# The third block's shared up products by seven products of eight, in a decoder layer kernel

## The chip, the cores and the metric

The kernel runs on one core of one Trainium2 chip, in fp32 throughout. The metric is the device time of one execution in microseconds (us), as a median of several runs. The engines are TensorE (PE, products; PEld is its loading of weights), VectorE (DVE), ScalarE (ACT), GpSimd (POOL) and SyncE (SP, which issues most transfers). Products land in PSUM, which PE writes and DVE and ACT read.

## The reference, cut to what matters

The program is one decoder layer on x of 8 sequences of 256 rows and 256 features, 2048 rows in all: causal self attention with 16 heads; three rounds of a GRU whose input is an attention over a context of 120 rows; and a feed-forward part with one shared expert and eight routed ones, of which each row uses two. A layer norm follows each. The change is in the shared expert:

```
def _mlp(x, w1, b1, w2, b2):
    h = gelu(einsum('bsd,di->bsi', x, w1) + b1)
    return einsum('bsi,id->bsd', h, w2) + b2
...
return x + _mlp(x, sh_w1, sh_b1, sh_w2, sh_b2) + moe_out
```

w1 is 256 x 1024 and w2 is 1024 x 256. The gelu is the tanh form.

## The kernel before, in words

Rows are worked on in 4 blocks of 512 (`X[i]`), with their transposed copies `XT[i]`: 128 partitions, 2 chunks of features (`dc`), 512 rows. In the shared expert a unit u is half a block, 256 rows, so units 4 and 5 are the third block, i = 2.

`up` (L1223) makes the hidden values of one unit: for each of 8 slices c of the hidden dimension, two products of 128x128 weights by 128x256 rows add into PSUM, and ACT takes the sum out with gelu and bias into `hT` (L1241). Two slices share one PSUM tile of the pool "big", which has two buffers of two banks each. `down_group` (L1244) adds 8 products over the slices for 128 rows into a tile of the pool "bk" (four buffers). `shared_up`, `shared_down` and `parts` call these for the shared expert. The pool of `hT` has two buffers.

Around it stand these parts, in order of time. `place` (L1047) computes for each row the slots of its two experts, and POOL scatters the rows into a table `xd` with indirect transfers, 8 per block (L1070). `tables` works out which expert each tile of gathered rows has. The shared units 0 to 3 follow. Then comes the loop over 21 tiles of routed rows (`tile_fetch`, `tile_weights`, `tile_turn`, `tile_up`, `tile_down`, `tile_store`), whose results go to a table `yd`, and a branch for two rare tiles that is skipped when they are empty. The tail does the shared units 4 to 7. In it `fetch_back(i)` has POOL gather the two expert rows of each row of block i (8 indirect transfers, L1365, into 16 buffers `y`), `take_back(i)` has DVE add them with their weights to `Z[i]` (8 operations, L1379), and `finish` does the last layer norm and the store:

```
shared_up(4)
fetch_back(0)
shared_up(5)
fetch_back(1)
take_back(0)
parts(4)
take_back(1)
shared_up(6)
```

The order of PE and ACT is as written throughout (`manual_schedule`). In the tail DVE and POOL are as written too. Between the first stage and the tail, DVE and POOL are ordered by a scheduler, which can move an instruction ahead of earlier ones that are not ready: the additions of the shared bias for units 4 to 7 (L1268), written just ahead of the expert loop, run at 677 to 682 us, before the routing of the last two blocks.

`wih_sb` and `whh_sb` (128 partitions, 2 x 768 values each) hold the GRU's weights. Before these are loaded they hold sums for the query and key projections of the attention, which are already done by seven products of eight (`project_part`), as are the value projections (`product`); the additions of products there are on DVE (L392, L466), the sums of operands on POOL (L307). PE last reads `wih_sb` at about 395 us and `whh_sb` at 661 us.

Of the kernel before, what the change touches and what calls it, by code (L numbers as in the profile page):

```python
# [10 lines left out]
F32 = mybir.dt.float32  # L11
I32 = mybir.dt.int32
U16 = mybir.dt.uint16
AF = mybir.ActivationFunctionType
ALU = mybir.AluOpType
# [6 lines left out]
NE, FF = 8, 1024  # L22
P = 128
DC = D // P
# [5 lines left out]
FC = FF // P  # L30
# [7 lines left out]
RT = 256  # L38
# [27 lines left out]
def decoder_kernel(  # L66
# [23 lines left out]
    nc = tc.nc  # L90
# [6 lines left out]
    def big(name):  # L97
        return pools["big"].tile([P, 2, 512], F32, tag="big", name=name)

    def bank(name):  # L100
        return pools["bk"].tile([P, 512], F32, tag="bk", name=name)
# [13 lines left out]
    XT = [act.tile([P, DC, BLK], F32, tag=f"XT{i}", name=f"XT{i}") for i in range(NBLK)]  # L115
# [52 lines left out]
    b1c = vec_sb[:, 0 : (NE + 1) * FC].rearrange("p (e c) -> p e c", c=FC)  # L168
# [10 lines left out]
    wih_sb = const.tile([P, DC, 3 * D], F32, name="wih_sb")  # L179
    whh_sb = const.tile([P, DC, 3 * D], F32, name="whh_sb")  # L180
# [28 lines left out]
    def load_shared():  # L209
        w1_sb = sh.tile([P, DC, FF], F32, name="sh1")  # L210
        w2_sb = sh.tile([P, FC, D], F32, name="sh2")
        nc.sync.dma_start(w1_sb, sh_w1.rearrange("(c p) f -> p c f", p=P))
        nc.sync.dma_start(w2_sb, sh_w2.rearrange("(c p) d -> p c d", p=P))
        return w1_sb, w2_sb
# [56 lines left out]
    with (  # L271
# [34 lines left out]
        def minus(o, a, b, op=ALU.subtract):  # L306
            nc.gpsimd.tensor_tensor(o, a, b, op)  # L307
# [335 lines left out]
        for k in range(last + 1):  # L643
            i, j = divmod(k, 2 * NPAIR)
# [46 lines left out]
    shared = load_shared()  # L691
# [8 lines left out]
    fh = ctx.enter_context(tc.tile_pool(name="fh", bufs=2, side="right"))  # L700
# [51 lines left out]
    for h in range(2):  # L752
        n = (NSINGLE + 1 - h) // 2
# [12 lines left out]
    def tt(o, a, b, op):  # L766
        nc.vector.tensor_tensor(o, a, b, op)  # L767
# [452 lines left out]
    f1 = ctx.enter_context(tc.tile_pool(name="f1", bufs=1))  # L1220
    wff = ctx.enter_context(tc.tile_pool(name="wff", bufs=2))

    def up(w1_sb, bias, rhs, name, width=RT, between={}):  # L1223

        hT = fh.tile([P, FC, RT], F32, tag="hT", name=f"hT_{name}")
        for c2 in range(FC // 2):
            between.get(c2, nothing)()
            ph = big(f"ph_{name}_{c2}")
            for a in range(2):
                c = 2 * c2 + a  # L1230
                for dc in range(DC):
                    nc.tensor.matmul(  # L1232
                        ph[:, a, 0:width],
                        w1_sb[:, dc, ts(c, P)],
                        rhs(dc),
                        start=dc == 0,
                        stop=dc == DC - 1,
                    )
            for a in range(2):
                c = 2 * c2 + a  # L1240
                nc.scalar.activation(hT[:, c, 0:width], ph[:, a, 0:width], AF.Gelu_apprx_tanh, bias=bias[:, c : c + 1])  # L1241
        return hT

    def down_group(po, w2_sb, hT, a):  # L1244
        for c in range(FC):
            nc.tensor.matmul(po, hT[:, c, ts(a, P)], w2_sb[:, c, :], start=c == 0, stop=c == FC - 1)  # L1246

    def down(w2_sb, hT, name, between=nothing, groups=RT // P):
        po = bank(f"pf_{name}").rearrange("p (a b) -> p a b", b=D)
        for a in range(groups):  # L1250
            if a:
                between()
            down_group(po[:, a, :], w2_sb, hT, a)
        return po
# [3 lines left out]
    HT = {}  # L1258

    def shared_up(u, between={}):  # L1260
        i, h = divmod(u, BLK // RT)
        rhs = lambda dc: XT[i][:, dc, ts(h, RT)]
        HT["s", u] = up(shared[0], b1c[:, NE, :], rhs, f"s{u}", between=between)

    def shared_bias(u):

        i, h = divmod(u, BLK // RT)
        nc.vector.scalar_tensor_tensor(  # L1268
            Z[i][:, ts(h, RT // P), :],
            X[i][:, ts(h, RT // P), :],  # L1270
            2.0,
            shared_b.unsqueeze(1).to_broadcast([P, RT // P, D]),
            ALU.mult,
            ALU.add,
        )

    def shared_down(u):

        i, h = divmod(u, BLK // RT)
        if u < SHARED_FIRST:  # L1280
            shared_bias(u)
        hT = HT.pop(("s", u))
        po = bank(f"pf_s{u}").rearrange("p (a b) -> p a b", b=D)
        down_group(po[:, 0, :], shared[1], hT, 0)
        yield
        down_group(po[:, 1, :], shared[1], hT, 1)
        z = Z[i][:, ts(h, RT // P), :]
        tt(z, z, po, ALU.add)
        yield
# [55 lines left out]
    def tile_down(t):  # L1345
        row = TI.pop(t)[0]
        w1_sb, w2_sb, bt, b2t, e = TW.pop(t)
        n = groups(t)
        po = down(w2_sb, HT.pop(("t", t)), f"t{t}", groups=n)
        yo = f2.tile([P, 2, D], F32, tag="yo", name=f"yo_{t}")[:, 0:n, :]  # L1350
        tt(yo, po[:, 0:n, :], b2t.unsqueeze(1).to_broadcast([P, n, D]), ALU.add)
        return row, yo
# [6 lines left out]
    def fetch_back(i):  # L1359

        for n in range(NSUB):
            for j, slot in enumerate(slots):
                g = i * NSUB + n
                y = f2.tile([P, D], F32, tag="y", name=f"y_{g}_{j}", bufs=NY)
                nc.gpsimd.indirect_dma_start(  # L1365
                    out=y,
                    out_offset=None,
                    in_=yd[:, :],
                    in_offset=bass.IndirectOffsetOnAxis(ap=slot[:, g : g + 1], axis=0),
                )  # L1370
                Y[g, j] = y
# [12 lines left out]

    nunit = NT // RT
    shared_up(0)
    place(1)
    residual(3)
    nc.scalar.preload_act_table_set(LNEXP)
    norm(2)  # L1390
    norm(3)
    part = [shared_down(u) for u in range(nunit)]

    def parts(u):
# [7 lines left out]

    route_logits(2, (0, 1))
    shared_up(
        1,
        {
# [14 lines left out]
    for u in range(2, SHARED_FIRST):  # L1421
        shared_up(u)
        if u == SHARED_FIRST - 1:
            tile_fetch(TILES[2])
            tile_weights(TILES[1])
            next(part[u])
            tile_turn(TILES[0])
            next(part[u])
        else:
            parts(u)  # L1430
    for u in range(SHARED_FIRST, nunit):
        shared_bias(u)


    with tc.manual_schedule(engines={mybir.EngineType.SP}):
        for k, t in enumerate(TILES):
# [5 lines left out]
            if k:  # L1442
                done = tile_down(TILES[k - 1])
# [19 lines left out]
    engines = {mybir.EngineType.PE, mybir.EngineType.Activation, mybir.EngineType.DVE, mybir.EngineType.Pool}  # L1463
    ctx.enter_context(tc.manual_schedule(engines=engines))
    half = NSUB // 2
    shared_up(4)
    fetch_back(0)
    shared_up(5)
    fetch_back(1)
    take_back(0)  # L1470
    parts(4)
# [16 lines left out]
    po = [bank(f"pf_s7_{a}")[:, 0:D] for a in range(half)]  # L1488
    hT = HT.pop(("s", 7))
    for a in range(half):  # L1490
        n = half + a
# [69 lines left out]
```

## Time and profile before

| | |
|---|---|
| median of 3 runs | 1056.69 us (1056.6 to 1056.99) |
| the profiled execution | 1092.43 us, its span 1090.4 us |
| PE busy | 1047.5 us, 96% of the span |
| DVE, ACT, POOL busy | 480.5, 422.9, 266.5 us |
| first product of unit 4's up | 1010.75 us |
| up of units 4 and 5 on PE | 14.05 us |
| POOL's gathers in the tail | 32, from 1014.28 us on |

All times of a view are us from the start of the span. A row of groups gives line, engine, operation, what it writes and reads with shapes, the count, then busy us and mean ns of one, and then how long the engine stood idle just before and what ended that. A row of the timeline gives start, length, engine, line, operation and count, and in brackets the idle time before it with its releaser. A row of the chain gives start, length and who worked. The trace records each fp32 product as two instructions, so a unit's 16 up products are x32. A product's record is longer than the step from one to the next, since they overlap in the pipeline: lengths of whole groups are used, not the mean of one.

### The profile page before, as it was taken

The page shows a single profiled execution, that of the slowest core. Times are in us where ns is not written, and L with a number is a line of the kernel's source. Part 1 is how long each engine was busy: PE and PEld are TensorE (multiplying, and loading weights), DVE is VectorE, ACT ScalarE, POOL GpSimd, SP SyncE. Part 2 cuts the span into 40 slices and gives each one's busy share as a digit, 9 for nine tenths or more (in the row PEclk, how much of TensorE's full clock was granted, in tenths as well). Part 3 has the DMA queues.
Part 4 walks back from the last instruction along what each step waited for, and adds up shares of the span by engine and source line. Part 5 has one row for each costly group of instructions (what it writes and reads, how often), then busy time and mean ns, then how long its engine had stood idle before and what let it go on. Part 6 is the DMA issues. An engine that isn't in the chain of part 4 may idle for free. (4 is left out here: it accounts for less than half of the span.)

```text
span 1090.4 us, 14560 instructions
## 1 busy us (share of the span) xinstructions
PE 1047.5 (96%) x5102; PEld 764.2 (70%) x5102; DVE 480.5 (44%) x1516; ACT 422.9 (39%) x1174; POOL 266.5 (24%) x314
## 2 busy tenths in 40 slices
PE   9999999999999999999999999959999999999877
PEld 5556766766676865555656667948888888888756
DVE  4567667766776362444434578510101010010137
ACT  2345555544467112555555444413223222221223
POOL 3734424444234032112121013330000000000650
PEclk9999999999999999999999999979999999999969
DMA  9000000000001089990000001153666766752231
GB/s 298 7 1 1 2 1 1 2 1 1 1 1 59 1 294 358 347 335 0 1 1 0 1 14 51 44 181 122 220 217 217 252 208 222 226 190 69 87 90 64
DMA packets 91368, 114.14 MB, mean 105 GB/s; under 512 B 6751, under 2 KB 82335, under 8 KB 91295
## 3 DMA queue, kind: packets, MB, share of 16 engines
q1 hardware_dynamic: 87135, 102.72, 28.8%
q0 software_dynamic: 3072, 8.39, 2.4%
q10 hardware_dynamic: 1088, 2.10, 0.5%
q8 instruction: 41, 0.67, 0.3%
q14 instruction: 32, 0.26, 0.1%
HBM read 67.97 MB, written 45.22 MB: 104 GB/s over the span
## 5 line engine op out<-in xcount | busy, mean ns | idle before, releaser
L503 ACT ACTIVATE sc<-sc,nmax 128x128 f32<-128x128 f32 (+1 forms) x256 | 113.3, 444 | 147.2 <-DVE nmax L490 147.2
L518 POOL TENSOR_TENSOR sc<-sc,sums 128x256 f32<-128x256 f32 (+1 forms) x128 | 103.2, 827 | 180.1 <-DVE sums L515 136.5
L1241 ACT ACTIVATE hT_t<-ph_t,bt 128x256 f32<-128x256 f32 (+1 forms) x168 | 66.3, 445 | 192.8 <-issue 138.3
L910 PE MATMUL gate<-XT,whh_sb 128*128 128x512 f32 x288 | 133.8, 593 | 0.0
L1232 PE MATMUL ph_t<-xgT,w 128*128 128x256 f32 (+1 forms) x672 | 132.5, 355 | 0.8 <-ACT hT_t L1241 0.8
L1246 PE MATMUL pf_t<-w,hT_t 128*128 128x256 f32 x592 | 131.1, 379 | 0.0
L1232 PEld LDWEIGHTS ph_t<-xgT,w 128*128 128x128 f32 x672 | 116.2, 190 | 14.8 <-ACT hT_t L1241 1.0
L1246 PEld LDWEIGHTS pf_t<-w,hT_t 128*128 128x128 f32 x592 | 111.0, 190 | 14.3
L1365 POOL DMA_INDIRECT y<-yd,slot x32 | 30.8, 961 | 308.8 <-ACT hT_s L1241 294.0
L910 PEld LDWEIGHTS gate<-XT,whh_sb 128*128 128x128 f32 x288 | 54.2, 189 | 48.5 <-issue 46.2
L392 DVE TENSOR_TENSOR qk<-pq,qk 128x256 f32<-128x256 f32 x168 | 64.7, 420 | 39.5 <-ACT qk L390 29.1
L490 DVE CUSTOM_DVE_ANT_0 sc<-pp,mask 128x128 f32<-128x128 f32 (+1 forms) x256 | 75.2, 349 | 8.6 <-PE pp L478 7.6
L1246 PE MATMUL pf_s<-sh,hT_s 128*128 128x256 f32 x256 | 61.3, 394 | 17.8 <-ACT hT_s L1241 11.6
L919 PEld LDWEIGHTS gate<-at,G 120*128 120x128 f32 x288 | 54.5, 189 | 29.9 <-issue 23.3
L919 PE MATMUL gate<-at,G 120*128 120x256 f32 x288 | 72.1, 379 | 0.4 <-DVE at L767 0.4
L1232 PE MATMUL ph_s<-XT,sh 128*128 128x256 f32 x256 | 62.1, 398 | 8.9 <-issue 6.8
L1337 DVE COPY xgT<-xg 128x512 f32<-128x512 f32 (+1 forms) x21 | 13.2, 628 | 128.5 <-PE xg L1336 128.5
L1246 PEld LDWEIGHTS pf_s<-sh,hT_s 128*128 128x128 f32 x256 | 50.0, 197 | 26.2 <-ACT hT_s L1241 12.0
L767 DVE TENSOR_TENSOR yo<-pf_t,b2t 128x512 f32<-128x512 f32 (+1 forms) x21 | 13.2, 628 | 121.5 <-PE pf_t L1246 121.5
L1241 ACT ACTIVATE hT_s<-ph_s,vec_sb 128x256 f32<-128x256 f32 x64 | 26.8, 471 | 96.3 <-PE ph_s L1232 54.0
L1232 PEld LDWEIGHTS ph_s<-XT,sh 128*128 128x128 f32 x256 | 50.2, 199 | 19.2 <-issue 9.8
L548 PE MATMUL po<-pT,v 128*64 128x256 f32 (+1 forms) x512 | 55.7, 339 | 2.6 <-ACT pT L537 2.6
(258 smaller groups left out, 1618.7 us busy)
## 6 DMA issues: line engine op xcount, KB each, us to landing
w<-in_ew_dram SPq DMA_DIRECT2D x42, 1024.0 KB, 5.6
xd<-zeros SPq DMA_DIRECT2D x1, 16640.0 KB, 54.8
yd<-zeros SPq DMA_DIRECT2D x1, 16640.0 KB, 103.2
xg<-xd SPq DMA_DIRECT2D x16, 256.0 KB, 5.1
yd<-yo SPq DMA_DIRECT2D x16, 256.0 KB, 5.8
b2t<-in_b_dram SPq DMA_DIRECT2D x21, 128.0 KB, 5.7
sh<-in_sh_w_dram SPq DMA_DIRECT2D x2, 1024.0 KB, 7.2
X<-in_x_dram SPq DMA_DIRECT2D x3, 512.0 KB, 11.6
```

Of the source, the lines that this page charges most:

```text
L392: nc.vector.tensor_tensor(o, pq[:, ts(n, S)], old, ALU.add)
L490: nc.vector.tensor_tensor_reduce(out=sc[:, h, seg[t]], in0=pp[h][:, seg[t]], in1=mask[:, seg[t]], scale=-(HD**-0.5), scalar=3.0e38, op0=AL ...
L503: nc.scalar.activation(sc[:, h, seg[t]], sc[:, h, seg[t]], AF.Exp, scale=-1.0, bias=nmax[:, t, h : h + 1], accum_out=sums[:, t, h : h + 1],)
L518: nc.gpsimd.tensor_tensor(sc[:, :, seg[t]], sc[:, :, seg[t]], sums[:, t, :].unsqueeze(2).to_broadcast([P, 2, w]), ALU.mult,)
L548: nc.tensor.matmul(po[ts(h, HD), q0:S], V[i][:, 2 * bi + c, ts(2 * pr + h, HD)], pT[:, h, 0:S] if c == 0 else pT[:, h, S:384], start=c == ...
L767: nc.vector.tensor_tensor(o, a, b, op)
L910: nc.tensor.matmul(pg[:, oc, :], whh_sb[:, dc, o], XT[i][:, dc, :], start=dc == 0, stop=not given and dc == DC - 1,)
L919: nc.tensor.matmul(pg[:, oc, ts(bi, S)], G[:, BPB * i + bi, o], AT_[p][:, bi, :], start=not hidden, stop=not hidden or bi == BPB - 1,)
L1232: nc.tensor.matmul(ph[:, a, 0:width], w1_sb[:, dc, ts(c, P)], rhs(dc), start=dc == 0, stop=dc == DC - 1,)
L1241: nc.scalar.activation(hT[:, c, 0:width], ph[:, a, 0:width], AF.Gelu_apprx_tanh, bias=bias[:, c : c + 1])
L1246: nc.tensor.matmul(po, hT[:, c, ts(a, P)], w2_sb[:, c, :], start=c == 0, stop=c == FC - 1)
L1365: nc.gpsimd.indirect_dma_start(out=y, out_offset=None, in_=yd[:, :], in_offset=bass.IndirectOffsetOnAxis(ap=slot[:, g : g + 1], axis=0),)
```

## The change

The two `shared_up` calls for block 2 are replaced by one `up_seven(2)`. The block's product is taken as 2 x 2 blocks: the weights by halves of the hidden dimension (512 wide) and the two chunks of features, the rows by the same two chunks and the two units. Seven products of sums of these blocks give the four results. `up_prepare(2)`, written after the shared biases and ahead of the expert loop, makes eight sums on POOL, s1 to s4 from the weights and t1 to t4 from the rows, in the space of `wih_sb` and `whh_sb`.

`up_seven` goes through four quarters q of 128 hidden values in each half. A quarter has two PSUM tiles of "big": x takes four products and y three. ACT copies the first product to SBUF (tile `c`, two buffers), DVE makes four additions of PSUM to `c`, and ACT takes the four results with gelu and bias into the `hT` of both units. `down_group` gets an order of slices, which for units 4 and 5 alternates between the halves. `fetch_back(0)` now stands after both units' up products, in the written order.

```
-    def down_group(po, w2_sb, hT, a):
-        for c in range(FC):
-            nc.tensor.matmul(po, hT[:, c, ts(a, P)], w2_sb[:, c, :], start=c == 0, stop=c == FC - 1)
+    def down_group(po, w2_sb, hT, a, order=range(FC)):
+        for n, c in enumerate(order):
+            nc.tensor.matmul(po, hT[:, c, ts(a, P)], w2_sb[:, c, :], start=n == 0, stop=n == FC - 1)
...
+    done = [w.rearrange("p k n -> p (k n)") for w in (wih_sb, whh_sb)]
+    up_sums = [done[0][:, ts(j, FF // 2)] for j in range(3)] + [done[1][:, 0 : FF // 2]]
+    half_sums = [done[1][:, FF // 2 + j * RT :][:, 0:RT] for j in range(4)]
+    up_blocks = [shared[0][:, k, ts(m, FF // 2)] for m in range(2) for k in range(DC)]
...
+    def up_prepare(i):
+        def minus(o, a, b, op=ALU.subtract):
+            nc.gpsimd.tensor_tensor(o, a, b, op)
...
+        minus(s1, a21, a22, ALU.add)
+        minus(t1, b12, b11)
+        minus(s2, s1, a11)
+        minus(t2, b22, t1)
+        minus(s3, a11, a21)
+        minus(t3, b22, b12)
+        minus(s4, a12, s2)
+        minus(t4, b21, t2)
...
+    def up_seven(i):
...
+        hT = [fh.tile([P, FC, RT], F32, tag="hT", name=f"hT_s{2 * i + n}") for n in range(2)]
+        for q in range(FC // 2):
+            c = f1.tile([P, 4, RT], F32, tag="up", name=f"up_{i}_{q}", bufs=2)
+            x, y = (big(f"up_{i}_{q}_{j}").rearrange("p a (b q) -> p (a b) q", q=RT) for j in range(2))
+            for j, (a, b) in enumerate(((a11, b11), (s3, t3), (a12, b21), (s2, t2))):
+                nc.tensor.matmul(x[:, j], a[:, ts(q, P)], b, start=True, stop=True)
+
+            nc.scalar.copy(c[:, 1], x[:, 0])
+            tt(c[:, 0:2], x[:, 2:4], c[:, 1:2].to_broadcast([P, 2, RT]), ALU.add)
+            tt(c[:, 3], x[:, 1], c[:, 1], ALU.add)
+            for j, (a, b) in enumerate(((s4, b22), (a22, t4), (s1, t1))):
+                nc.tensor.matmul(y[:, j], a[:, ts(q, P)], b, start=True, stop=True)
+            tt(c[:, 1:3], y[:, 0:2], c[:, 1:4:2], ALU.add)
+            tt(c[:, 1:4:2], y[:, 2:3].to_broadcast([P, 2, RT]), c[:, 1:4:2], ALU.add)
+            for n in range(2):
+                for m in range(2):
+                    k = q + m * FC // 2
+                    nc.scalar.activation(
+                        hT[n][:, k, :], c[:, 2 * m + n], AF.Gelu_apprx_tanh, bias=b1c[:, NE, k : k + 1]
+                    )
+        for n in range(2):
+            HT["s", 2 * i + n] = hT[n]
...
+    BY_HALVES = [k + m * FC // 2 for k in range(FC // 2) for m in range(2)]
...
-        down_group(po[:, 0, :], shared[1], hT, 0)
+        order = BY_HALVES if u // 2 == 2 else range(FC)
+        down_group(po[:, 0, :], shared[1], hT, 0, order)
         yield
-        down_group(po[:, 1, :], shared[1], hT, 1)
+        down_group(po[:, 1, :], shared[1], hT, 1, order)
...
     for u in range(SHARED_FIRST, nunit):
         shared_bias(u)
+    up_prepare(2)
...
-    shared_up(4)
+    up_seven(2)
     fetch_back(0)
-    shared_up(5)
     fetch_back(1)
```

More of the change, by code (lines that the diff above doesn't have):

```diff
@@ L1263, in shared_up @@
         HT["s", u] = up(shared[0], b1c[:, NE, :], rhs, f"s{u}", between=between)
+    done = [w.rearrange("p k n -> p (k n)") for w in (wih_sb, whh_sb)]
[5 more added lines that the diff above has]
+            nc.gpsimd.tensor_tensor(o, a, b, op)
+        a11, a12, a21, a22 = up_blocks
+        s1, s2, s3, s4 = up_sums
+        b11, b12, b21, b22 = (XT[i][:, k, ts(n, RT)] for k in range(DC) for n in range(2))
+        t1, t2, t3, t4 = half_sums
+        minus(s1, a21, a22, ALU.add)
[6 more added lines that the diff above has]
+        minus(t4, b21, t2)
@@ new lines, in up_seven @@
+    def up_seven(i):
+        a11, a12, a21, a22 = up_blocks
+        s1, s2, s3, s4 = up_sums
+        b11, b12, b21, b22 = (XT[i][:, k, ts(n, RT)] for k in range(DC) for n in range(2))
+        t1, t2, t3, t4 = half_sums
+        hT = [fh.tile([P, FC, RT], F32, tag="hT", name=f"hT_s{2 * i + n}") for n in range(2)]
[19 more added lines that the diff above has]
+            HT["s", 2 * i + n] = hT[n]
```

## The prediction

> **What bounds the kernel now.** I read the page first, then the chain of waits in order of time, then windows of 10 us, then the timeline of the tail. TensorE (PE) is busy 96% of the span, and the chain that ended last runs on it through the whole tail: the up products of units 4 and 5 together, the down products of unit 4, then up 6, down 5, up 7; only from 1070 us does it leave PE for the last layer norms.
>
> ```profile
> 1010.75 14.05 PE ph_s L1232 x64
> 1024.80 5.83 PE pf_s L1246 x27
> ...
> 1047.48 9.03 PE ph_s L1232 x28
> 1056.52 6.91 PE pf_s L1246 x32
> 1063.42 6.92 PE ph_s L1232 x32
> 1070.34 0.02 issue
> 1070.37 0.84 ACT hT_s L1241 x2
> ```
>
> The reader should see the first line: it is what the change rewrites. The trace counts each fp32 product twice, so x64 is 32 products, 0.439 us each (14.05 / 32).
>
> The "..." above hides a stall that belongs to the profile and not to the time. The windows show two of them (columns: busy us and instructions of PE, PEld, DVE, ACT, POOL, then clock, DMA share, GB/s):
>
> ```profile
> 710.00:720.00 10.00, 1.15 (x5) 0.66 (x4) 2.58 (x13) 0.84 (x2) 7.56 (x9) 0.76 0.29 105
> 720.00:730.00 10.00, 6.30 (x18) 5.16 (x19) 0.00 (x0) 0.84 (x2) 0.33 (x1) 0.56 0.56 183
> ...
> 1030.00:1040.00 10.00, 3.01 (x8) 1.52 (x8) 0.00 (x0) 0.84 (x2) 7.56 (x9) 0.80 0.36 104
> 1040.00:1050.00 10.00, 4.86 (x10) 2.88 (x10) 1.56 (x4) 0.35 (x1) 3.43 (x5) 0.50 0.20 62
> ```
>
> In both, POOL issues its indirect transfers without a pause while PE, DVE and ACT hardly run. Sizes: the down products of unit 2 start at 708.13 and end at 730.77, where 32 instructions take 7.07 us elsewhere: 15.6 lost. Down 4 and up 6 run from 1024.64 to 1056.52, where 64 take 13.98 elsewhere: 17.9 lost. The profiled execution took 1092.43 (span 1090.4 and 2.0 around it); without 33.5 it is 1058.9, and the median is 1056.69. So the timed runs have next to nothing of these stalls, PE is the bound in them almost from end to end, and I reckon against 1056.69, with a tail in which PE runs on: up 4 and 5 at 1010.75 to 1024.8, down 4 to 1031.8, up 7 done near 1052.5.
>
> **What is removed and added on PE.** Two `shared_up` calls of 16 products become 4 quarters (q) of 7: 28 for 32 products, all 128x128 by 256 columns as before, so 4 x 0.439 = 1.76 us is the most that can come off (0.17%).
>
> **What is added on the other engines, and the loop it makes.** Before, ACT took each product pair out of PSUM straight into `hT`, and DVE had no part in it. Now each quarter needs one ACT copy, four DVE additions and four Gelu, in a chain. The kernel already has additions of this kind in its projections, so the prices are rows of this trace:
>
> ```profile
> L392 DVE TENSOR_TENSOR qk<-pq,qk 128x256 f32<-128x256 f32 x168 | 64.7, 420 | 39.5 <-ACT qk L390 29.1 <-PE pq L387 6.5 <-DVE qk L392 0.5
> ...
> L466 DVE TENSOR_TENSOR v<-pv,v 128x512 f32<-128x512 f32 x42 | 28.5, 687 | 6.1 <-PE pv L454 5.5
> ...
> L1241 ACT ACTIVATE hT_s<-ph_s,vec_sb 128x256 f32<-128x256 f32 x64 | 26.8, 471 | 96.3 <-PE ph_s L1232 54.0 <-issue 19.7 <-remote 16.6
> L555 ACT COPY ot<-po 128x256 f32<-128x256 f32 x64 | 22.5, 351 | 15.8 <-PE po L548 15.8
> ```
>
> ACT's order is copy(q), four Gelu(q), copy(q+1), and the last two Gelu wait for DVE's last addition. So copy(q+1) waits for the end of quarter q, and a quarter can't be shorter than: copy 0.35, additions of 512, 256, 512 and 512 elements 0.68 + 0.40 + 0.68 + 0.68, two Gelu 0.84 (a pair in the timeline), and about 0.15 for the handing over (0.03 from ACT to DVE and back, 0.02 to 0.04 between additions): **3.8 us**. PE's share of a quarter is 7 x 0.439 = 3.08; the old code's, 8 x 0.439, was 3.52. The loop, not PE, sets the pace, and it is slower than the old PE work.
>
> PE feels it through the PSUM pool "big", which has two buffers: x(q) and y(q). The four products into x(q+1) wait until the third reader of x(q), the 256-element addition, is done; those into y(q+1) wait for the last addition of q, which is earlier. Worked from PE's first product at 0 (0.22 us from a product's last issue to the reader, as from PE to the first Gelu in the timeline): x(0) issued at 1.76, copy done 1.5, additions at 2.66 and 3.1, y(0) at 3.08, additions at 3.8 and 4.5, last Gelu 5.4. x(1) starts at 3.2 and is there at 4.9, but copy(1) ends only at 5.8, its two additions at 6.95; x(2) starts at 7.05, and x(3) one period later at 10.85. PE leaves at 10.85 + 3.08 = **13.93, against 14.05: 0.1 us gained**, and the other 1.6 us of the saving is waiting. It starts late (the first quarter is free) and therefore isn't a loss.
>
> Down 4 does not add a wait: its order by halves (0, 4, 1, 5, 2, 6, 3, 7) needs q=3 only for its seventh product, 13.9 + 6 x 0.44 = 16.5, and the two Gelu it needs end near 14.6 and 15.7. What I can't read from the trace is whether the halves c[1] and c[3], written as one strided output, are kept apart from c[2] between them. If not, one Gelu more stands in the loop (4.2 us a quarter) and PE leaves at 14.75: 0.7 lost. With 0.05 to 0.1 us more at each of the eight handovers, the loss is 0.7 to 1.0 in place of the 0.1 gained. The ends of this step are -1.76 (loop hidden) and +1.0; I take **+0.3**, near the worked value and a little to the bad side, since each unknown here adds.
>
> The clock: PE now pauses up to 0.7 us per quarter. In 660 to 670 us PE was busy 8.10 of 10 us with pauses up to 1.7, and the granted clock stayed 1.00; I charge nothing.
>
> **What moves behind it.** DVE: the 8 multiply-adds of `take_back(0)` (0.48 each) ran in the old order at 1017 to 1026.5 as their rows landed; now they queue behind 16 additions and run from about 1026 to 1030.5. Waiting for them are the addition of down 4's result (PE done 1031.8) and, through the 16 y buffers, the 17th gather on POOL:
>
> ```profile
> 1033.14 0.95 POOL L1365 DMA_INDIRECT y<-yd,slot  x1 [0.30 <-issue]
> ...
> 1049.76 1.07 POOL L1365 DMA_INDIRECT y<-yd,slot  x1 [5.66 <-DVE Z L1379]
> ```
>
> It issues at 1033.1, 2.6 us after they are done: no cost; without that cover a late gather would hold up `take_back(2)` and the end one for one. `fetch_back(0)` is now written after both up units, but `up_seven` puts nothing on POOL or SP, so no transfer moves. ACT needs no table for the copy (at 686.16 a copy stands between two Gelu with no load). `down_group`'s order costs nothing.
>
> **The sums.** Eight POOL additions: four of 512 elements at 1.27 and four of 256 at 0.73 (both in the rows of L307) are 8.0 us. They need the tables that the recurrent stage has done with (661) and block 2's transposed rows (679.2), and no one reads them before 1010. POOL's queue there:
>
> ```profile
> 683.40 0.96 POOL L1070 DMA_INDIRECT xd<-X,slot  x1 [0.30 <-issue]
> 700.41 0.95 POOL L1070 DMA_INDIRECT xd<-X,slot  x1 [16.04 <-DVE slot L1066]
> ```
>
> The hole of 16 us holds them, or they run after 720, where POOL idles for 294 us: cost nothing. Behind them on POOL stand the 16 scatters to 720.3; the first expert's row fetch waits for these, so sums in front of a scatter that is ready would cost up to their own 8 us. One rule speaks against the hole. The Trainium skill, "SBUF — State Buffer", section "Who interferes with whom", says that a DVE instruction with two SBUF inputs and a GpSimd instruction that reads SBUF take one shared port in turn, and the later one is fully blocked. DVE's routing in 688 to 700, many such additions of 0.19, computes the slots that the scatters wait for. By the rule the four weight sums, if they run there, can push the scatters by up to 5.1 us; by the row (a hole, and the others ready by 688) by nothing. I found no row here with DVE blocked by POOL, so I take 0 and keep 5 in the tail.
>
> **Sum:** 1056.69 + 0.3 + 0 + 0 = **1057.0**.
>
> **Rivals.** *The loop is hidden (8%)*: if Gelu and copy overlap better than their order says, PE runs at 3.08 a quarter: 1054.9 to 1055.3, still inside 0.2%. *A second wait in the loop (17%)*, the one on the other side: if PE holds x(q+1) back until y(q) is read out, the period is x 1.76 + y 1.32 + 1.58 of additions = 4.66 from the first quarter on, PE leaves at 17.05, and the time is 1059.7; with slow handovers and the strided halves not kept apart, 16.1 and 1058.8. It decides from a period of about 4.4 us on (3.08 + 3 x 4.4 is 2.1 over 14.05). For it: two buffers only, and 0.7 us of wait already; against it: nothing in the old trace waits for a buffer that it doesn't write. *The sums in front of the scatters or the routing (6%)*: +2 to +8, 1059 to 1065. *The stall comes earlier in timed runs too (6%)*: in the profile ACT falls behind from 1023 on; a PE that depends on ACT and DVE there would stop 8 us sooner: 1065 if timed runs had the stall, against which stands the 33.5 us reckoning. *Something unnamed over 0.2% faster (3%) or slower (2%)*: no step has 2.1 us to give.
>
> **How the numbers follow.** The likeliest case (58%) spans 1056.4 to 1057.8. 0.2% is 2.1 us, about what a measurement of this kernel can tell from no change. Slower by more: half of the 17%, the 6 and the 6, and 2: 0.23. Faster: 0.03. Same: 58, 8 and the other half of 17, 0.74. The range 1055.0 to 1059.8 takes in the hidden loop and the second wait and leaves out the two 6% cases, the 3 and the 2.
>
> **What would show it.** The up stage on PE should hold 56 instructions of `up_seven` in 13.5 to 15 us, with waits of about 0.7 before x(2) and x(3) put down to DVE; DVE three additions at 0.68 and one at 0.40 in each quarter; ACT's copy right behind a Gelu. The eight sums should stand on POOL away from the scatters, and the first scatter of block 2 still near 700.4. The prediction is wrong if PE's wait per quarter is over 1.3 us, if a scatter starts later, or if the up stage is under 12.8 us.

## The result, and the profile after

The changed kernel takes **1058.3 us** (median of 22 runs, 1057.96 to 1058.66) against 1056.68 for the kernel before (22 runs beside it, 1056.47 to 1057.43): 1.0015 times as long, with an interval of 1.0009 to 1.0021. It is 1.6 us slower: within the 0.2% (2.1 us) that the prediction took for no change, though the interval excludes 1. Seven products in place of eight did not pay here.

On some chips the executions of either kernel, timed or profiled, have the two long stalls that the prediction saw in the profile of before and take some 1080 to 1100 us, on others they have none and take 1056 to 1059 (but for one of before, 3229.82): the profile of before is of the first kind, the recorded times and the profile of after (1058.06 us, span 1056.4) are of the second. So only stretches outside the stalls can be compared between these two profiles. No profile of before without the stalls exists; the kernel with "sums of one column" below, which has before's up products, stands for it where one is needed.

The chain that ended last, after (start, length, who worked; the lines that answer to the "x64" line of before):

```profile
993.27 1.98 PE up L1301 x8
...
995.27 0.38 ACT up L1303
...
995.68 0.70 DVE up L767
...
996.41 0.43 DVE up L767
...
1004.90 1.97 PE up L1301 x8
...
1035.82 0.84 ACT hT_s L1241 x2
```

Before, PE alone carried this stretch. Now the chain leaves PE after the first four products, goes over ACT's copy and DVE's additions, and comes back to PE only at 1004.90, with the last quarter. The timeline of PE gives the three waits (in brackets: idle time and what ended it):

```profile
996.98 0.67 PE L1301 MATMUL up<-XT,sh 128*128 128x256 f32 x2 [0.44 <-DVE up L767]
...
1000.94 0.67 PE L1301 MATMUL up<-XT,sh 128*128 128x256 f32 x2 [0.70 <-DVE up L767]
...
1004.90 0.67 PE L1301 MATMUL up<-XT,sh 128*128 128x256 f32 x2 [0.70 <-ACT hT_s L1313]
...
1008.00 7.07 PE L1246 MATMUL pf_s<-sh,hT_s 128*128 128x256 f32 x32
```

They are the first products into x(1), x(2) and x(3), and then the start of down 4. From the first up product (993.27) to that start is **14.73 us**. The same stretch of before is 1010.75 to 1024.64, 13.89 (the 14.05 of the chain's line includes the length of the last product), so a product costs 13.89 / 32 = 0.434, 28 cost 12.15, and the new stage loses 2.6 us of PE. The idle times in brackets are 1.84 of it; they count from the end of a product's record, which is longer than the 0.434 of its step.

Of the additions themselves the groups say (busy us, mean ns of one, then the idle time before and its releaser):

```profile
L767 DVE TENSOR_TENSOR up<-up,up 128x512 f32<-128x512 f32 x12 | 8.3, 692 | 6.3 <-ACT up L1303 5.7
L767 DVE TENSOR_TENSOR up<-up,up 128x256 f32<-128x256 f32 x4 | 1.7, 424 | 0.1
L1303 ACT COPY up<-up 128x256 f32<-128x256 f32 x4 | 1.4, 356 | 15.1 <-PE up L1301 15.1
```

0.69, 0.42 and 0.36 us: the prices taken from the projections were right. The windows where the profile of before has its stalls (PE, PEld, DVE, ACT, POOL busy us and instructions, then PE's clock, DMA share, GB/s) show a PE that never pauses:

```profile
710.00:720.00 10.00, 10.00 (x48) 8.81 (x47) 0.69 (x1) 2.52 (x6) 6.64 (x7) 1.00 0.55 207
720.00:730.00 10.00, 10.00 (x50) 8.79 (x50) 1.38 (x2) 1.48 (x4) 0.00 (x0) 1.00 0.84 274
```

The sums on POOL's timeline, with the hole that the prediction named (s4 first, then the four sums of rows, then the next scatter):

```profile
660.77 1.26 POOL L1275 TENSOR_TENSOR whh_sb<-sh,wih_sb 128x512 f32<-128x512 f32 x1 [1.05 <-PE gate L910]
...
682.49 1.42 POOL L1275 TENSOR_TENSOR whh_sb<-XT 128x256 f32<-128x256 f32 x2
683.86 1.53 POOL L1275 TENSOR_TENSOR whh_sb<-XT,whh_sb 128x256 f32<-128x256 f32 x2
698.51 0.98 POOL L1070 DMA_INDIRECT xd<-X,slot  x1 [13.12 <-DVE slot L1066]
```

Three more sums ran at 393.9 to 397.7; the DVE and PE operations there have the same lengths as with sums of one column. The first scatter of block 2 again starts right behind the routing (hole of 13.12 and 2.9 of sums ahead of it, 16.04 before), and the 21 tiles of experts take 265.89 us in both kernels. The sum at 660.77 looks as harmless as the others; it is not, as a later experiment shows.

### The profile page after: what moved, and what is told of

The parts are those of the page before. It is cut to its first block, busy times and chain, and to the rows that moved or that the text cites. A ratio compares the mean times of both kernels' runs of the same rounds, so it can differ in the third digit from the quotient of the medians.

```text
span 1056.4 us, 14585 instructions
## 1 busy us (share of the span) xinstructions
PE 1037.6 (98%) x5094; PEld 759.0 (72%) x5094; DVE 490.1 (46%) x1532; ACT 425.3 (40%) x1178; POOL 274.6 (26%) x322
## 5 line engine op out<-in xcount | busy, mean ns | idle before, releaser
L564 PE MATMUL py<-wo_sb,ot 128*128 128x256 f32 x256 | 57.5, 379 | 0.0
L1246 PE MATMUL pf_s<-sh,hT_s 128*128 128x256 f32 x256 | 57.0, 379 | 0.0
L533 PE MATMUL pt<-ident,sc 128*128 128x128 f32 x384 | 56.0, 282 | 0.0
L548 PEld LDWEIGHTS po<-pT,v 128*64 128x64 f32 x512 | 31.0, 136 | 33.5 <-issue 17.6
```

The costliest lines, as they stand in the source:

```text
L533: nc.tensor.transpose(pt[:, ts(c, P)], sc[:, h, ts(c, P)], ident)
L548: nc.tensor.matmul(po[ts(h, HD), q0:S], V[i][:, 2 * bi + c, ts(2 * pr + h, HD)], pT[:, h, 0:S] if c == 0 else pT[:, h, S:384], start=c == ...
L564: nc.tensor.matmul(py, OT[i][:, pr, ts(n, P)], wo_sb[:, pr, :], start=pr == 0, stop=pr == NPAIR - 1)
```

## The experiments

Edits are against the changed kernel unless said. Chips 15, 5 and 0 have the stalls, chip 12 has not. What was measured is the up stage (start of its first product to start of the first product of down 4) in each profile, and the time where it says something.

**The two kernels once more, on chips 15 and 5.** Both unedited; first before, then after, then before.

> The kernel before, once more, for a profile that may be without the two long stalls. Time 1056.7. The changed kernel's trace shows its up stage on PE at 14.73 us against 14.05, which is 0.68 of the 1.62 us by which it is slower. If the other 0.94 us lies in the tail too, this profile shows it there as a stretch that is shorter than in the changed kernel; if it lies elsewhere, the expert loop (265.89 us in both traces so far) or the stretch before it is shorter.

> The changed kernel once more, beside the other three on one chip. On a chip without the two stalls: 1058.3 with an up stage of 14.7 us. On one with the stalls (the last four runs had them, in the timed executions as well), the stage should still be 14.7, and if ACT and DVE fall behind before PE has left it, as the rival of the earlier stall says, the time is 3 to 8 us above the kernel before; otherwise within 2 of it.

> The kernel before, for a trace without the stalls, to place the 0.94 us of the loss that the up stage leaves open. Theory 'a longer end': the stretch from the end of unit 7's up products to the end of the span is 0.5 to 0.9 us shorter than in the changed kernel (20.8 there). Rival 'earlier in the program': the start of the expert loop comes 0.9 us earlier than at the 727.4 of the changed kernel.

Before took 1090.54 us (22 runs, chip 15) and 1091.79 (14 runs, chip 5), each within its interval of no difference from the runs of before beside it; its up stage is 13.89 in both profiles. After took 1094.07 (22 runs), a ratio of **1.0032 (1.0017 to 1.0047)**, 2.9 us more; its up stage is 14.72, with the same waits of 0.44, 0.70 and 0.70. So the stalls are not a matter of profiling (the 1056.7 expected for before did not come on these chips), and the stage itself is as long with them as without. What the stalls add is seen in PE's timeline of after on chip 5, right behind the up stage:

```profile
1022.50 3.39 PE L1246 MATMUL pf_s<-sh,hT_s 128*128 128x256 f32 x14
1033.22 6.95 PE L1246 MATMUL pf_s<-sh,hT_s 128*128 128x256 f32 x18 [7.33 <-issue]
```

Down 4 stops after its seventh product (x14): the eighth needs a Gelu that ends at 1033.17, held up behind a DVE addition that starts only at 1031.93. In before's profile on the same chip x25 of its 32 instructions run without a break; they need only Gelu that ran earlier. That PE stops sooner when ACT and DVE fall behind is the prediction's rival "the stall comes earlier". After is 1.3 us dearer here than without stalls, not the 8 us that were put down for it. Not all of that need come from the tail: from the gate products at 657 us to the next layer norm's products (L221) PE takes 21.92 us in this profile and 19.79 in before's on the same chip, a stretch in which one of the sums runs (below). How the 2.9 us divide is not shown.

**The sums alone.** The old up products, with the eight sums still made (nothing reads them) and the new order of down 4.

```
-    up_seven(2)
+    shared_up(4)
     fetch_back(0)
+    shared_up(5)
     fetch_back(1)
```

> The changed kernel with the old up products of units 4 and 5 put back, and the eight sums on POOL kept, though no one reads them. Theory 'all of the loss is in the tail': 1056.7, no difference to the kernel before. Rival 'the sums cost the 0.9 us that the up stage does not explain': 1057.6.

The up stage is 13.89 again, so nothing of it comes from the sums. The time was 1088.26 us (6 runs), 0.997 of before (0.9958 to 0.9983); against stalls of some 33 us, which differ from run to run, that is no reading of a 2 us effect, and the next one shows the same. So neither expectation can be told from these times. The end of this profile is 0.4 us longer than before's, which was not expected; it is taken up below.

**The copy ahead of the last Gelu.** The Gelu of quarter q are written behind the copy of q+1, so that ACT's copy no longer waits for the end of the quarter before.

```
             nc.scalar.copy(c[:, 1], x[:, 0])
+            prev()
...
-            for n in range(2):
-                for m in range(2):
...
+            prev = partial(gelus, q, c)
+        prev()
...
```

> The changed kernel, but ACT's copy of quarter q+1 stands ahead of the four Gelu of quarter q, so that the copy no longer waits for DVE's last addition and two Gelu. Theory 'the loop copy, four additions, two Gelu sets the pace': PE waits hardly at all, the up stage falls from 14.7 to 12.3 to 12.7 us, time 1058.3 - 2.2 = 1056.1. Rival 'two PSUM buffers set the pace' (the third reader of x and the last reader of y, whatever ACT does): the stage stays at 14 to 14.7 and the time at 1057.6 to 1058.3.

**The copy twice**, the same copy a second time, to make the loop longer by a known amount.

```
             nc.scalar.copy(c[:, 1], x[:, 0])
+            nc.scalar.copy(c[:, 1], x[:, 0])
```

> The changed kernel with ACT's copy of each quarter made twice over. Theory of the loop: each of the three later quarters starts 0.35 us later on PE, the up stage is 15.8 us and the time 1059.3 to 1059.4. Rival 'the copy lies in the shadow of PE's products and DVE alone sets the pace': under 0.2 us more, 1058.3 to 1058.5.

PE's timeline with the copy first:

```profile
1011.81 0.67 PE L1310 MATMUL up<-XT,sh 128*128 128x256 f32 x2 [0.44 <-DVE up L767]
...
1019.27 0.67 PE L1310 MATMUL up<-XT,sh 128*128 128x256 f32 x2 [0.50 <-DVE up L767]
...
1022.37 3.19 PE L1246 MATMUL pf_s<-sh,hT_s 128*128 128x256 f32 x14
```

With the start at 1008.11 that is 14.26 us: 0.46 less than after, in the rival's 14 to 14.7, where a loop on ACT alone would have given back nearly all. A wait of 0.44 to 0.50 stays ahead of every quarter. With the copy twice the quarters are 4.11, 4.36 and 4.36 us apart and the stage is 15.93 (15.8 expected), +0.40 for each of three quarters: the copy lies in PE's chain in every quarter, the first as well. Together: **two chains hold PE**. One is x's own: four products, then the copy, an addition of 512 and one of 256, and only then is x free (3.71 us a quarter). The other is the loop through the Gelu (3.96), which costs 0.25 more from the second quarter on. Times of the two: 1088.04 (5 runs, 0.9962, 0.9949 to 0.9975) and 1096.33 (22 runs, 1.0046, 1.0035 to 1.0057). The first has few runs on a stalling chip and stands beside the 0.997 of the sums alone, so it is not taken as a gain.

**y out of the way**, so that x has both large buffers: y is put in the pool "bk", in two tiles of one bank.

```
-            x, y = (big(...) for j in range(2))
+            x = big(f"up_{i}_{q}")...
+            y, y2 = (bank(f"up_{i}_{q}_{j}")... for j in range(2))
...
-                nc.tensor.matmul(y[:, j], a[:, ts(q, P)], b, start=True, stop=True)
+                nc.tensor.matmul((y, y, y2)[j][:, (0, 1, 0)[j]], a[:, ts(q, P)], b, start=True, stop=True)
...
```

> The changed kernel with the three products of y in two tiles of the other PSUM pool, so that x has both buffers of its own and PE need not wait for the additions on x(q) before x(q+1). ACT's order is left as it is. Theory 'ACT's in-order loop alone sets the pace of the results': PE runs ahead, leaves the up products sooner (13 to 13.6 us), but down 4 then waits for the last Gelu, which stay at their place: 0.5 to 0.9 us gained in all, 1057.5. Rival 'the PSUM buffers alone': up 12.3 us and no wait in down 4, 2.3 us gained, 1056.0.

**Both**, the copy first and y out of the way.

> Both edits: ACT's copy of q+1 ahead of the Gelu of q, and x with two buffers of its own. If these are the two waits of PE and there is no third, PE does the 28 products in 12.3 to 12.6 us without a wait, down 4 follows at once, and the time is 2.1 to 2.4 us below the changed kernel: 1056.0, or 0.7 below the kernel before. If a third wait stands behind them (DVE has 2.7 us a quarter against PE's 3.1, so it should not be DVE), the stage stays above 13.3.

With y out of the way PE has no wait between the quarters (12.48 us, of which 0.15 idle ahead of down 4), near the rival's 12.3. ACT's loop is still there, its copies 4.03 to 4.06 us apart against PE's quarters of 3.02, but now it reaches PE only in down 4, with two waits of 0.46 and 0.55, as the theory had it. With both it is **12.16, the 28 products at full pace**:

```profile
1006.04 0.67 PE L1311 MATMUL up<-XT,sh 128*128 128x256 f32 x2
...
1018.20 3.19 PE L1246 MATMUL pf_s<-sh,hT_s 128*128 128x256 f32 x14
1023.05 4.15 PE L1246 MATMUL pf_s<-sh,hT_s 128*128 128x256 f32 x18 [1.66 <-ACT hT_s L1301]
```

The 1.66 falls in the stall; on chip 12 (below) the stage is 12.16 as well, and down 4 follows and runs without a break. So PE's waits in the stage come from the PSUM buffers, ACT's order makes them longer, and nothing else holds PE there. On chip 5, with its stalls, the times of the two were 1090.1 (14 runs, 0.9995, 0.9985 to 1.0006) and 1088.97 (14 runs, 0.9987, 0.9974 to 0.9999).

**Without stalls: sums of one column, both, and after.** The first is before's up products with the eight sums cut to one column each; its results are not used. The other two are as above.

```
-            nc.gpsimd.tensor_tensor(o, a, b, op)
+            nc.gpsimd.tensor_tensor(o[:, 0:1], a[:, 0:1], b[:, 0:1], op)
```

> The up products of the third block as before, and the eight additions on GpSimd kept in their place but cut to one column each, so that they take next to no time; nothing reads their results. Six profiles so far have 20.69 to 21.02 us from the first product of the last down stage to the end of the span wherever the eight additions are in the program, and 20.24 to 20.29 in the three without them. Theory (it is the number of instructions in the program that moves the end, not what the additions do): 20.7 to 20.8 here too, with an instruction transfer at the end of the span, and about 1.7 us around the span in place of 1.9. Rival (the additions' own work, or the tables that they write, delays something): 20.24 to 20.3 and 1.9.

> The copy first and y in its own banks, once more. Its up stage takes 12.16 us where before takes 13.89. Where the cores run without the two long stalls of PE, VectorE and ScalarE around the bursts of indirect transfers, theory (the gain on PE is a gain in time, less 0.3 at the program's end): 1.4 us below before, 1055.3, ratio 0.9987. Rival (the Gelu that are late at the start of the next stage take the gain back): within 0.5 us of before. Where the stalls are there: 0.9987 as before, with an interval that takes in no difference.

> The changed kernel once more, beside the kernel before and beside the version with both waits taken away. Where the cores run without the two long stalls: 1.2 to 1.6 us above before, ratio 1.0015. Where the stalls are there: 1.0032 as in the run before, since the up stage ends in a PE that depends on ScalarE and VectorE when these fall behind.

These three ran on chip 12, where before takes 1056.81. After took **1058.24** (21 runs, 1.0013, 1.0006 to 1.002), +1.43. The sums of one column took 1056.99 (10 runs, 1.0001, 0.9992 to 1.001), +0.18 and not to be told from nothing. Both waits taken away took **1056.0** (13 runs, 0.9992, 0.9984 to 1.0000), 0.8 below before, where 1.4 was expected.

A part of what after costs beyond its up stage lies at 661 us. The timelines of POOL, DVE and PE, after on chip 12:

```profile
660.67 1.26 POOL L1275 TENSOR_TENSOR whh_sb<-sh,wih_sb 128x512 f32<-128x512 f32 x1 [1.03 <-PE gate L910]
...
660.80 1.18 DVE L767 TENSOR_TENSOR hot<-hot,rank 128x32 f32<-128x32 f32 x1
...
674.85 1.71 PE L221 MATMUL xt<-ident,X 128*128 128x128 f32 x8 [0.59 <-DVE X L250]
```

and with sums of one column:

```profile
660.99 0.19 DVE L767 TENSOR_TENSOR hot<-hot,rank 128x32 f32<-128x32 f32 x1
...
674.75 1.68 PE L221 MATMUL xt<-ident,X 128*128 128x128 f32 x8 [0.30 <-DVE X L250]
```

A DVE addition of 32 columns, 0.19 us by itself, takes 1.18 beside the sum and ends 0.05 us after it (661.98 and 661.93). That is the rule of the Trainium skill which the prediction weighed ("SBUF — State Buffer", "Who interferes with whom": a DVE instruction with two SBUF inputs contends with a GpSimd instruction that reads SBUF, for ports that are an exclusive lock), in this trace and with a number: 0.99 us. Most of it is taken up by slack, and 0.29 reach PE: 0.59 in place of 0.30. The profile of after on the result's chip has the same (1.18 and 0.57). With stalls it is worse: on chip 5 another addition of the routing (`pb`) takes 1.03 beside the sum, and PE's wait for ACT's `z` a little later is 2.62 in place of 1.75.

**The sums later.** Both waits taken away, and the sums held back behind the last scatter by a one-column copy that reads a result of the last down product before the expert loop.

```
-    up_prepare(2)
+    with tc.manual_schedule(engines={mybir.EngineType.Pool}):
+        up_prepare(2)
...
+        nc.gpsimd.tensor_copy(s1[:, 0:1], Z[1][:, NSUB - 1, 0:1])
         minus(s1, a21, a22, ALU.add)
```

> The version with both waits taken away, and the eight additions on GpSimd moved behind the last scatter: a one-column copy ahead of them reads the result of the last down product before the expert loop, so that they run from about 728 us, where VectorE has one copy or addition in several us. In the run before, one of the sums (660.67 us, 1.26 long) ran beside VectorE's routing, a two-input addition of 32 columns there took 1.18 us and not 0.19, and PE waited 0.59 us and not 0.30 for the layer norm behind it. Theory (the wait of 0.29 is the sum's, through VectorE): that addition back at 0.19, PE's wait at about 675 us back at 0.30, everything behind it 0.29 earlier; time 1055.7, 1.1 below before where the cores run without the two long stalls. Rival (the delay at 661 to 675 us comes from elsewhere, or the gathers do not start earlier): the wait stays at 0.59 or the end stays, 1056.0. The sums' new place can cost something too, if a VectorE operation of the expert loop is held up there; PE has 7 us between its needs of VectorE, so nothing is expected.

The sums ran at 738.5 to 746.2. The timelines of DVE and PE:

```profile
660.91 0.19 DVE L767 TENSOR_TENSOR hot<-hot,rank 128x32 f32<-128x32 f32 x1
...
674.67 1.72 PE L221 MATMUL xt<-ident,X 128*128 128x128 f32 x8 [0.30 <-DVE X L250]
```

Both are back at 0.19 and 0.30, so the 0.29 us were the sum's. The run fell to a chip with stalls (chip 0): 1081.26 us against 1085.26 (6 and 10 runs, 0.9965, 0.9953 to 0.9977). That is 4.0 us faster there; how much of it holds where there are no stalls was not run.

**Where both's gain ended.** Its up stage on chip 12 is 12.16, 1.73 under before. The sum at 661 us, which both still has, takes 0.29 of it back. The stretches behind the stage take 0.34 more, against the kernel with sums of one column on the same chip: 0.14 ahead of down 6, which waits, and 0.20 from there to DVE's last operation (17.41 us; 17.21 there). With 0.18 at the end of the program this makes 0.9, where 0.8 was measured. Its chain that ended last, in the tail:

```profile
996.72 0.98 POOL y L1430
...
1016.10 2.80 DMA y<-yd,slot
...
1019.35 0.48 DVE Z L1444
```

It runs over the first 16 of POOL's 32 gathers, issued one every 1.25 to 1.3 us from 996.7 on, and from there over DVE and the layer norms to the end; PE is in it only up to 996.46. In the profiles of before, after, sums of one column, both and sums later the first gather starts 3.53 to 3.55 us after the first up product, however long the up stage is. So the gathers hang on the end of the expert loop, and by this chain a still shorter up stage would not bring the end of this kernel forward.

**The end of the program.** From the start of DVE's last operation to the end of the span are 3.16 us in before, 3.71 in after, 3.67 with both, 3.61 with sums of one column, 3.63 with the sums alone, and 3.17 with the sums later. What lies around the span is 1.94 us in before and 1.70 to 1.73 in the others. The net is +0.2 to +0.3 by the traces, and +0.18 by the times of the sums of one column, which can't be told from nothing. In after and with sums of one column a transfer of instructions (queue q14) stands at the end of the span. The DMA view of after, 1055.8 to 1056.4 us:

```profile
q14 instruction: 1, 0.01, 4.6%
```

In before the last such transfer comes 1.9 us behind the span's end; with the sums later none comes there. But with the sums alone the end is as long, and the transfer comes some 0.2 us behind the span. And the sums later have one instruction more than both, and the short end. So neither the transfer inside the span nor the number of instructions explains the longer end by itself. The sums of one column show that the additions' work is not needed for it; its cause stays open.

## Why the prediction was right or wrong

The likeliest case said 1057.0, and it is 1058.3: inside the range and within 0.2% of before, but 0.5 beyond the span of the likeliest case (1056.4 to 1057.8), and +1.6 where +0.3 was summed. That the range held is in part luck: its slow side was there for the second wait, which did not come. The likeliest case was missed by three terms that all came out on the slow side, the up stage mis-sized and two that were put at nothing or not named. The sum 1056.69 + 0.3 + 0 + 0 becomes, with what was measured, + 0.84 + 0.29 + 0.18 = +1.3; measured were +1.6 and +1.4, and what is left is smaller than the intervals (the 0.18 for its part can't be told from nothing).

| step | predicted | measured |
|---|---|---|
| most that PE can save | 1.76 | 1.73 (both: 13.89 to 12.16) |
| up stage | -1.76 to +1.0, taken +0.3 | **+0.84** |
| waits before x(2), x(3), period less seven products | about 0.7 each, DVE | 0.92 each (3.96 less 3.04; idle time 0.70), DVE and ACT |
| wait before x(1), in the same terms | 0.1 (3.2 less 3.08) | **0.67** (3.71 less 3.04; idle time 0.44) |
| period of the loop | 3.8 | 3.96 |
| `take_back(0)` behind the additions | 0 | 0: gathers 1.25 to 1.45 apart, without a break |
| the sums | 0, up to 5.1 in the tail | **0.29** |
| the clock | 0 | 0: granted 1.00 in every window of 10 us, 0.999 over the span |
| the end of the program | not named | +0.18, not clear of nothing (0.2 to 0.3 by the traces) |

*The loop.* The mechanism was right: ACT and DVE set the pace, PE waits for x's third reader. What was mis-sized is the step "copy done 1.5". It let the copy start behind x's second product; in the profile it starts at 2.00 us after the stage's start, behind the fourth. Why it waits for products that it doesn't read was not tested. The copy is done at 2.37, the two additions at 3.11 and 3.57, and x(1) starts at 3.71 and not at 3.2: 0.5 us. The period of 3.96 in place of 3.8 gives 0.3 more. The "0.1 gained" was besides reckoned on unequal terms, a start of a product against the end of one (14.05 in place of 13.89). The two strided halves are kept apart from the half between them: ACT's Gelu of the half between starts with the fourth addition, at 997.66, and not behind it, so the worse case of 4.2 a quarter did not come.

*The sums.* "By the row (a hole, ...) by nothing" failed: 0.29 us where 0 was taken. The place was one reason. The hole at 684 to 700 is as free as predicted, but the prediction put all sums there or later, and the scheduler put one at 660.77, the moment PE had read `whh_sb` for the last time. There DVE was at the second block's routing, and the rule that the prediction set aside is the one that held. The other reason is the words "no row here with DVE blocked by POOL". The routing of before has no POOL addition beside it, but another place has one, beside a layer norm:

```profile
386.73 1.90 POOL L856 TENSOR_TENSOR sq<-XT 128x1024 f32<-128x1024 f32 x1
...
387.31 1.33 DVE L244 SCALAR_TENSOR_TENSOR step<-mv,rstd 128x4 f32<-128x4 f32 x1
```

The DVE operation has two inputs in SBUF, a median of 0.16 us over its 14 records, and here it ends 0.01 us after POOL's. This row of the trace spoke for the rule before the change was made. One of the prediction's signs of being wrong came, in small: the first scatter of block 2 starts 0.27 us later than with the sums moved (41.52 against 41.25 us from the gate products at 657).

*The stalls.* "A stall that belongs to the profile and not to the time" was wrong as a statement: it belongs to the chip. The bookkeeping on it was right (1058.9 by taking 33.5 us off, for 1056.69), since the recorded times are those of a chip without it. The rival "the stall comes earlier", which was said to need stalls in timed runs, is seen in the profile where they are, with +2.9 us for after and +5.5 for the copy twice in all. What makes PE, DVE and ACT stall on some chips while POOL issues indirect transfers stays open; no run here varied it.

*The rivals.* The loop was not hidden, and PE did not wait for y. The second wait of that rival exists as x's own chain, 3.71 a quarter, well short of the 4.4 from which it would have decided (3.08 + 3 x 4.4 is 2.2 over 14.05, not 2.1, which shifts that limit by 0.03).

## What to carry to other kernels

A PSUM tile that takes several products and has several readers holds its buffer from the first product to the last reader: add the products, the copy and the additions in a row and compare with PE's work on both buffers. Here the copy had to be counted from the tile's last product, though it reads only the first. When products are traded for additions, look for the new bound in the buffers and in the order of the engine that does two jobs; giving the two tiles separate buffers and putting the copy first brought the whole 1.73 us of PE here, and the end then hung on the gathers and on DVE, so that 0.8 was left. An operation that is "free" on GpSimd has to be looked up by where the scheduler puts it: an addition of 1.26 us there cost a two-input addition on DVE 0.99.

## What the runs showed that was not expected

- A 512-column addition on GpSimd held up a 32-column addition on DVE from 0.19 to 1.18 us; 0.29 us of it reached PE (on a chip with stalls one wait of PE grew by 0.87), and it went away when the sum was moved.
- The same kernel takes 1056.7 us on some chips and 1085 to 1092 on others; most of the difference lies in the stretches of two bursts of indirect transfers. A profile from one and times from another can't be set against each other without that.
- With eight additions of one column each in the program, the end of the span is 0.45 us longer than in before (3.61 against 3.16) and what lies around it 0.2 shorter.
